# Four places for residual rows, attention-time norms on GpSimd, and a last query block whose exponents are all split in PSUM

## The chip, the cores and the metric

The kernel runs on one core of a Trainium2 chip. The metric is the device time of one execution, in microseconds (us); the median of three runs stands for a kernel. The engines are called as in the profile: PE (TensorE, with its weight loads as PEld), DVE (VectorE), ACT (ScalarE), POOL (GpSimd) and SP (SyncE, which here only issues DMAs).

## The reference

`x` has shape (2, 2048, 512), `cond` (2, 512). A transformer block with conditioned norms is followed by a graph attention over the label mask `adj` of shape (2, 2048, 2048, 11). Cut to what matters here:

```python
# transformer block
h = _ada_ln(x, cond, Wln1, bln1)          # layer norm * (1 + scale) + shift, from cond
q, k, v = heads(h @ Wq + bq), heads(h @ Wk + bk), heads(h @ Wv + bv)   # 16 heads of 32
attn = softmax(einsum('bhqd,bhkd->bhqk', q, k) / sqrt(32))             # 2048 x 2048
x = x + einsum('bhqk,bhkd->bhqd', attn, v).reshape(B, L, D) @ Wo + bo
h = _ada_ln(x, cond, Wln2, bln2)
x = x + gelu(h @ W1 + b1) @ W2 + b2       # 512 -> 2048 -> 512
# graph attention: every row attends to the first 20 rows of its batch, in two directions,
# with a bias and a gate from the 11 labels; then output = x + relu(self_feat + both directions)
```

## The kernel before

**How instructions come into order.** The program is written as straight Python, but every engine call goes through a recorder, the class `Order`. For each call it notes what the call reads and writes. `flush()` then plays a list scheduler over all recorded operations: an operation is taken when its inputs are ready by a table of costs (`cost()`) and latencies between engines, the lowest recorded index first within 100 ns. Operations on DVE and POOL that use the port which the two share are planned one after the other, and POOL is made to wait for the DVE operation ahead of it there. The planned order is then what each engine's queue holds, and the chip runs each queue strictly in that order, whatever the real durations are. All instructions are issued from one line of `flush()`, so every row of the profile says L271, and instructions are told apart by the names of their tiles. In the cost table a `tensor_scalar` on POOL stands at `161 + 0.833 * n` ns, which is 588 ns for a row of 512; on DVE it is 455 ns with two pointers as operands.

**Places.** Tiles are mapped by tag to rings of fixed SBUF places (`places()`). The tag "xr" has two, `vf0` and `vf1`. A third tile of that tag has to wait until the first is read out. The tags "el" and, later, the MLP's raw weights "wr" share places (`el2`, `el3`), as do the MLP's "gl" and the places `h4`, `h5`.

**Attention.** There are 32 heads (two batches of 16). A head has 4 query blocks of 512 and 16 key tiles of 128, taken as 32 units of two key tiles. N is the count of all units. For a unit u:

- `scores`: PE writes two score tiles `st` (128 x 512) into one of three PSUM banks each.
- `exponents`: for the first 14 key tiles of a query block ACT writes the exponent to SBUF (`e`, in places `q0` to `q2`).
- `high_parts`: every 4 units a DMA issued by POOL casts `e` to its f16 high part `eh`.
- `low_parts`, 9 units later (LOW): `el = e - eh`, in f16, one share of the columns on DVE and the rest on POOL (0.52 on DVE, 0.8 in the last head).
- `weigh`, 11 units later (WEIGH): PE multiplies `eh` and `el` with the values `va` into the bank `av`.
- For the last two key tiles of a query block (INBANK = 2) the exponent stays in PSUM: ACT casts the high part, DVE subtracts the low part (tile `ep`), and `weigh_apart` does the products 5 units later (XLAG).

At the end of a query block DVE sums and normalizes `av` into `os`, which SP stores. For the next head the row maxima's bounds are made meanwhile: PE makes `mx`, ACT takes `ab`, DVE takes `sums` and `m`; in `largest_rows` POOL makes `hl`, DVE transposes it to `tr`, and SP sends it to the next head's queries.

**Work beside attention.** Each unit also takes some steps of a `Background` generator, with a pace per head. Heads 0 to 16 project the rest of batch 0 and norm and project batch 1 (`second_batch`: four blocks of 512 rows, each with `first_norm`). Heads 17 to 27 make the MLP's modulation, the output weights, the output projection of batch 0 with the residual (`output`), and the second norm of the MLP's first block (`second_norm`). Heads 28 to 31 do the output of batch 1's first twelve heads. `norm_block` subtracts the mean and multiplies by the reciprocal deviation, four rows-tiles of 128 x 512 a block, in place:

```python
V.tensor_scalar(r, r, mv[:, t, 0:1], rs[:, t:t + 1], ALU.subtract, ALU.mult)
```

Then PE transposes the result (`misc<-ident,x`). In `output`, a row tile `xr` of 128 x 512 is loaded one step ahead, POOL adds the bias, DVE adds the projection, and SP stores it (`x<-xr` in the profile); its place is free when the store has landed:

```python
xr = sb("xr", [P, D], F32, f"xr_{b}_{groups[0]}_{t}")
Q.dma_start(out=xr, in_=x[b, ts(t, P), :] if 0 in groups else x1_dram[i][r, :])
```

**After attention** the MLP takes eight blocks of 512 rows, each with its `second_norm`, with the labels and the folded graph weights made beside it; then the graph attention takes 16 pieces.

Of the kernel before, what the change touches and what calls it, by code (L numbers as in the profile page):

```python
# [11 lines left out]
F32 = mybir.dt.float32  # L12
F32R = mybir.dt.float32r
F16 = mybir.dt.float16
# [3 lines left out]
ALU = mybir.AluOpType  # L18
# [4 lines left out]
P = 128  # L23
# [6 lines left out]
NT = S // P  # L30
# [18 lines left out]

INBANK = 2  # L50
XLAG = 5

PACES = {0: 0.9, 1: 1.25, 17: 0.8, 18: 0.5, 27: 0.6}
NEG = 9000000000000000.0
# [312 lines left out]
def places():  # L367

    w = lambda *ranges: [f"w{i}" for a, b in ranges for i in range(a, b)]
    h = lambda *ranges: [f"h{i}" for a, b in ranges for i in range(a, b)]  # L370
    el = [f"el{i}" for i in range(4)]
    q = [f"q{i}" for i in range(3)]
    plan = {

        "raw": q, "wv": [f"v{i}" for i in range(4)], "wg_a": w((5, 7)),
        "wg_b": ["w1"], "x_a": w((7, 9), (2, 4)), "vs_a": ["w4", "eh2", "w0"],
        "hh0": h((0, 4)), "hl0": h((4, 8)),
        "hh1": ["eh0"], "hl1": ["eh1"], "ones": ["el2"],
        "squares": ["l0"], "g_c": ["l1"], "g_b": ["l2"], "w2": ["vf0", "ab0", "el0", "el1"],
        "bnd": ["h9"], "mag": ["el3"], "part": ["eh2"], "mod_row": ["w9"],  # L380

        "va": w((2, 4), (0, 2)), "va_rest": ["l2", "l3"], "el": el,
        "ab": ["ab0", "ab1"], "sums": ["l0"], "os": ["l4", "l5"],
        "vs": w((4, 5)), "bv": ["vf1"], "bo": w((6, 7)), "qk2": w((15, 17)), "u2": ["h9"],
        "wg": w((5, 7)), "x": w((7, 9)), "uf": ["l1"], "ep": ["ep0", "ep1"],
        "m2": ["m2_0", "m2_1"], "m1": ["m1_0", "m1_1"], "tr": ["tr_0", "tr_1"],
        "m3": ["m3_0", "m3_1"], "mv": ["mv_0", "mv_1"], "rstd": ["rstd_0", "rstd_1"],
        "bn": ["bn_0", "bn_1"],

        "wo": [f"v{i}" for i in range(4)], "xr": ["vf0", "vf1"], "ob": ["h8", "h9"],  # L390
        "oo2": w((15, 17)), "x1_a": w((7, 9)), "ob_b": ["l0"], "oo2_b": ["v2"],

        "w": w((4, 6), (7, 9), (2, 4), (14, 15), (11, 13), (9, 10), (15, 17), (10, 11), (13, 14),
               (0, 2)),
        "w8": ["eh0", "eh1"], "w16": q, "gh": h((0, 4), (8, 9)), "gl": h((4, 8), (9, 10)),
        "x1": ["v0", "v1"], "wr": ["ab0", "ab1"] + el[2:4], "gf": el[0:2],
        "g2": ["eh2"], "b2": w((6, 7)), "res": el[2:4] + ["ab0", "ab1"],

        "wbl": ["l0"], "ai": ["l1", "vf0", "vf1"], "af": ["l2"], "cv": ["l3"], "lab1": ["l4", "l5", "l6", "l7"],
        "cvt": ["v3"], "oo": ["v2"],  # L400
        "fw": ["vf0", "vf1"], "fv": ["ab0", "ab1"], "fs": ["v2"], "fq": ["l0", "l1", "l2", "l3"],
        "ws": w((4, 6)), "wq": h((0, 2)), "ft": h((2, 4)),
        "kbd": ["l4", "l5", "l6", "l7"], "gc": ["l4", "l5", "l6", "l7"], "kv": ["v3"], "kh": ["m1_0", "m1_1"],

        "x2t": ["vf0", "vf1", "ab0", "ab1"], "oos": ["l0", "l1", "l2", "l3"], "sc": ["v0", "v1", "v2"],
        "rwr": ["v3"], "gar": ["h2"], "gmx": ["mv_0", "mv_1"], "gsm": ["tr_0", "tr_1"], "o": el[2:4],
    }
    return plan
# [3 lines left out]
def transformer_then_graph_attention(  # L412
# [267 lines left out]

    HOLD = "hold"

    def norm_block(ps, xt, ln, b, name, hi, lo, stats=None):


        if stats is None:
            for mv, rs in statistics(lambda t: xt[t // 2][:, t % 2, :], 4, name):
                yield
        else:
            mv, rs = stats  # L690
        for t in range(4):
            r = xt[t // 2][:, t % 2, :]
            V.tensor_scalar(r, r, mv[:, t, 0:1], rs[:, t:t + 1], ALU.subtract, ALU.mult)
            if t % 2:
                yield
        for c in range(KC):
            pt = ps()
            for t in range(4):
                T.transpose(pt[:, ts(t, P)], xt[t // 2][:, t % 2, ts(c, P)], ident)
            A.activation(pt, pt, AF.Identity, bias=mods[:, ln, KC + c, b:b + 1],  # L700
                         scale=mods[:, ln, c, b:b + 1])
            split(hi(c), lo(c), pt, A, V)
            yield HOLD if c == 0 else None
# [10 lines left out]
    def first_norm(b, tb, ps, xt, fast, to, stats=None):  # L714
        to[b, tb] = features(b, tb, tb % 2 if fast else 0, "")
        hi, lo = to[b, tb]
        yield from norm_block(ps, xt, 0, b, f"a{b}_{tb}", lambda c: hi[c], lambda c: lo[c],
                              stats)
        for v in range(2 if b == 0 else 0):
            if fast and tb % 2:  # L720
                Q.dma_start(out=h_dram[b][tb][v].rearrange("c p t -> p c t"), in_=whole[v].bitcast(F32))
            else:
                for c in range(KC):
                    Q.dma_start(out=h_dram[b][tb][v, c], in_=to[b, tb][v][c].bitcast(F32))
# [137 lines left out]
    gates = {}  # L862
    pe = {}
    va, m2s, sts, avs, mxs = {}, {}, {}, {}, {}
    es, ehs, els, parts = [], [], {}, {}

    def put(dst, src, low):

# [81 lines left out]

    def split_tiles(u):

        return min(2, max(0, NT - INBANK - u % 8 * 2))

    def exponents(i):
        u = i // 2
        if i % 2 >= split_tiles(u):
            st = sts.pop(i)
            gates[u] = A.activation(st, st, AF.Exp, scale=SCALE)
            t = parts[i] = sb("ep", [P, 2, TB], F16, f"ep_{i}")  # L960
            split(t[:, 0], t[:, 1], st, A, V)
            return
        gates[u] = A.activation(es[u // EQ % 3][:, u % EQ, ts(i % 2, TB)], sts.pop(i), AF.Exp,
                                scale=SCALE)

    def high_parts(i):

        n = sum(split_tiles(i * EQ + k) for k in range(EQ)) * TB
        e, eh = (t[i % 3].rearrange("p u c -> p (u c)") for t in (es, ehs))
        G.dma_start(out=eh[:, 0:n], in_=e[:, 0:n])  # L970

# [18 lines left out]
                     stop=stop and q == 3, skip_group_check=True)  # L990

    def weigh_apart(u):
        for i in range(2 * u + split_tiles(u), 2 * u + 2):
            t = parts.pop(i)
            with order.together("PE"):
                add(avs[0], u // NU, i % NT, t[:, 0], t[:, 1])

    def weigh(u):
        n, qb, kp = u // NU, u % NU // 8, u % 8
        b, h = heads[n]  # L1000
        g, hh = h // 4, h % 4
        nt = split_tiles(u)
        if nt == 0:
            return
        last = kp == 7 or split_tiles(u + 1) == 0
        eh, el = ehs[u // EQ % 3][:, u % EQ], els.pop(u)
        if kp == 0:
            avs[0] = bank("av", [P, 4, VC + 1], F32, f"av_{n}_{qb}")
        av = avs[0]
        with order.together("PE"):  # L1010
            for a in range(nt):
                add(av, n, 2 * kp + a, eh[:, ts(a, TB)], el[:, ts(a, TB)], kp == a == 0,
                    last and a == nt - 1)
        if not last:
            return
        o = sb("os", [P, 4, HD], F32, f"os_{n}_{qb}")
        V.tensor_reduce(o, av[:, :, 1:VC].rearrange("p q (v d) -> p q d v", v=2), AX.X, ALU.add)
        rec = av[:, :, VC]
        V.reciprocal(rec, av[:, :, 0])
        V.tensor_tensor(o, o, rec.unsqueeze(2).to_broadcast([P, 4, HD]), ALU.mult)  # L1020
        Q.dma_start(
            out=o_dram[b][g][ts(qb, TB), ts(hh, HD)].rearrange("(t p) f -> p t f", p=P), in_=o)
# [30 lines left out]
    def attend(n, work=None):  # L1053

        for u in range(n * NU, (n + 1) * NU):
            i, m = u % NU, u + NU
            for a in range(2):
                exponents(2 * u + a)
                if 2 * u + a + 3 < 2 * N:
                    scores(2 * u + a + 3)  # L1060
# [5 lines left out]
                largest(m)  # L1066
            if u % EQ == 0 and u:
                high_parts(u // EQ - 1)
            if u >= LOW:
                low_parts(u - LOW)  # L1070
            if u >= WEIGH:
                weigh(u - WEIGH)
            if u >= XLAG:
                weigh_apart(u - XLAG)
            if m < N and i in (NU // 2 - 1, NU - 1):
                largest_rows(n + 1, i // (NU // 2))
            loads(u)
# [17 lines left out]
    def output(ps, b, groups, bo_b, tail=""):  # L1095
# [3 lines left out]
        def loaded(t):  # L1099
            i, r = b * NTB + t // 4, ts(t % 4, P)  # L1100
            ob = sb("ob" + tail, [P, ng, P], F32, f"ob_{b}_{groups[0]}_{t}")
            for k, g in enumerate(groups):
                Q.dma_start(out=ob[:, k, :], in_=o_dram[b][g][ts(t, P), :])
            xr = sb("xr", [P, D], F32, f"xr_{b}_{groups[0]}_{t}")
            Q.dma_start(out=xr, in_=x[b, ts(t, P), :] if 0 in groups else x1_dram[i][r, :])
            return ob, xr

# [90 lines left out]
    def second_norm(ps, i, xtag):  # L1198
# [6 lines left out]
        def new(to, name):  # L1205
# [1 line left out]
            return to[-1]  # L1207

        yield from norm_block(ps, xt, 1, i // NTB, f"m{i}", lambda c: new(hi, "gh"),
                              lambda c: new(lo, "gl"))  # L1210


    h1 = {}
# [124 lines left out]
    for u in range(N - WEIGH, N):  # L1338
        if u + WEIGH - LOW < N:
            low_parts(u + WEIGH - LOW)  # L1340
        weigh(u)
        if u + WEIGH - XLAG < N:
            weigh_apart(u + WEIGH - XLAG)
    work.rest()


# [483 lines left out]
```

## Time and profile before

| | |
|---|---|
| median of three runs | 3217.29 us (3211.15, 3221.28, 3217.29) |
| the profiled execution | 3220.79 us, of which the profile's span is 3219.0 us |
| mean granted TensorE clock in it | 0.986 |
| PE busy | 3055.7 us, 95% |
| DVE, ACT, POOL busy | 75%, 66%, 43% |
| attention | to about 2126 us |
| MLP and what runs beside it | from there to about 2910 us |
| graph attention | from there to the end |

A row of the timeline is: start, duration, engine, line, operation, output from inputs, the shape, the number of instructions merged into the row, and in brackets how long the engine had been idle before it and what ended that. A row of the form view gives the shortest, median and longest duration in ns. "PEclk" is the share of full speed that the clock gate granted. Busy times of PE are modelled ends of pipelined matmuls.

### The profile page before, as it was taken

What the parts mean: (1) busy time and instruction counts of PE and PEld (TensorE: products, weight loads), DVE (VectorE), ACT (ScalarE), POOL (GpSimd) and SP (SyncE); (2) the same over time, 40 slices, a digit from 0 to 9 for tenths busy, and PEclk for the clock granted to TensorE, in tenths of its full rate; (3) what the DMA queues carried; (4) which work ended last, traced back from release to release, by engine and by line L of the source; (5) the groups of instructions that cost most, each with busy time, mean ns of one, the idle gap of its engine ahead of it and who ended that gap; (6) DMA issues with size and microseconds to landing.
All of it is one profiled execution on the core that took longest, in us unless ns stands there. A gap on an engine that the chain in (4) does not pass through costs nothing.

```text
span 3219.0 us, 75753 instructions
## 1 busy us (share of the span) xinstructions
PE 3055.7 (95%) x28042; PEld 2096.1 (65%) x28042; DVE 2421.9 (75%) x5508; ACT 2132.2 (66%) x4233; POOL 1376.2 (43%) x1440
## 2 busy tenths in 40 slices
PE   7999989999999999999989989989999999999999
PEld 5555555555556555555555555568888887789998
DVE  6688878988889999899989999875576534235665
ACT  5788889999999999999989999842112212112221
POOL 2154545555555666666666656641000000002232
PEclk9999999999999999999999999999999999999999
DMA  8889998797979888899888778874122134132111
GB/s 287 248 210 257 246 227 215 175 227 174 207 169 212 185 173 182 180 205 203 190 187 176 163 150 192 190 222 145 29 66 67 60 105 150 29 98 78 64 58 55
DMA packets 353313, 519.33 MB, mean 161 GB/s; under 512 B 127407, under 2 KB 233431, under 8 KB 336558
## 3 DMA queue, kind: packets, MB, share of 16 engines
q0 software_dynamic: 36864, 234.90, 37.8%
q1 hardware_dynamic: 316078, 279.59, 28.3%
q8 instruction: 220, 3.60, 0.4%
q14 instruction: 151, 1.24, 0.1%
HBM read 187.97 MB, written 91.45 MB: 87 GB/s over the span
## 4 chain that ended last, share of the span: by engine, by line
PE 46%; ACT 4%; DVE 3%; issue 2%; DMA 2%; POOL 1%; SPq 0%; ACTq 0%; POOLq 0%; DVEq 0%
PE ph L271 11%; PE po_s L271 8%; PE gp L271 5%; PE misc L271 5%; PE av L271 4%; PE st L271 4%; PE gs L271 4%; PE mx L271 3%; PE po_x L271 3%; ACT e L271 2%; ACT ab L271 1%; DVE el L271 1%; PE pg L271 1%; DVE sums L271 1%; POOL el L271 1%
## 5 line engine op out<-in xcount | busy, mean ns | idle before, releaser
L271 POOL TENSOR_TENSOR el<-e,eh 128x496 f16<-128x496 f32 (+1 forms) x896 | 991.4, 1120 | 541.2 <-DVE el L271 201.5
L271 ACT ACTIVATE e<-st 128x512 f32<-128x512 f32 x1792 | 1040.7, 643 | 80.8 <-PE st L271 48.3
L271 DVE CUSTOM_DVE_ANT_0 sums<-mx,ab 128x512 bf16<-128x512 f32 x1024 | 700.1, 684 | 146.2 <-ACT ab L271 119.0
L271 PE MATMUL st<-qst,kst 98*128 98x512 f16 x2048 | 698.5, 385 | 50.3 <-DVE ep L271 20.2
L271 DVE TENSOR_TENSOR el<-e,eh 128x528 f16<-128x528 f32 (+1 forms) x896 | 735.2, 845 | 5.8 <-DMA eh<-e 3.0
L271 ACT ACTIVATE ab<-mx 128x512 f32<-128x512 f32 x1024 | 662.3, 647 | 42.3 <-PE mx L271 39.5
L271 PEld LDWEIGHTS <-eh 128*128 128x128 f16 x7168 | 468.3, 97 | 144.8 <-issue 95.1
L271 PE MATMUL av<-va,el 128*128 128x33 f16 x7168 | 510.7, 179 | 25.8 <-DVE el L271 18.2
L271 PE MATMUL av<-va,eh 128*128 128x65 f16 x7168 | 531.9, 192 | 2.5 <-DVE os L271 2.1
L271 PEld LDWEIGHTS <-el 128*128 128x128 f16 x7168 | 438.5, 96 | 129.0 <-DVE el L271 39.8
L271 PE MATMUL mx<-kst,qst 96*128 96x512 f16 x1024 | 388.7, 382 | 27.0 <-DVE m L271 24.3
L271 PE MATMUL mx<-ust,qst 96*128 96x512 f16 x1024 | 391.7, 383 | 21.6 <-ACT ab L271 13.8
L271 ACT ACTIVATE gf<-ph,b_c 128x512 f32<-128x512 f32 x128 | 88.2, 689 | 467.8 <-PE ph L271 411.8
L271 PEld LDWEIGHTS <-qst 96*128 96x128 f16 x2048 | 195.5, 98 | 288.7 <-issue 169.6
L271 PE MATMUL ph<-gh,w 128*128 128x512 f32 x1024 | 344.1, 398 | 3.8 <-ACT w L271 2.8
L271 PEld LDWEIGHTS <-kst 98*128 98x128 f16 x2048 | 168.1, 99 | 220.2 <-issue 173.5
L271 PE MATMUL po_s<-w,g 128*128 128x512 f32 x1152 | 295.6, 397 | 0.0
L271 POOL TENSOR_TENSOR res<-res,b_b 128x512 f32<-128x512 f32 x32 | 42.2, 1337 | 513.7 <-DVE g L271 243.3
L271 PEld LDWEIGHTS po_s<-w,g 128*128 128x128 f32 x1152 | 213.8, 188 | 48.4 <-issue 0.8
L271 DVE CAST g<-gf 128x512 fp32r<-128x512 f32 x128 | 56.0, 438 | 250.1 <-PE po_x L271 240.0
L271 POOL DMA_DIRECT2D eh<-e x256 | 145.9, 570 | 186.5 <-ACT e L271 88.2
L271 PEld LDWEIGHTS ph<-gh,w 128*128 128x128 f32 x1024 | 191.8, 188 | 49.0 <-ACT w L271 3.3
(259 smaller groups left out, 4642.0 us busy)
## 6 DMA issues: line engine op xcount, KB each, us to landing
eh<-e POOLq DMA_DIRECT2D x128, 1024.0 KB, 8.2
eh<-e POOLq DMA_DIRECT2D x128, 768.0 KB, 7.9
wg<-w SPq DMA_DIRECT2D x50, 512.0 KB
x<-in_x SPq DMA_DIRECT2D x24, 512.0 KB
qst<-qk SPq DMA_DIRECT2D x192, 64.0 KB
kst<-qk SPq DMA_DIRECT2D x192, 64.0 KB
x<-xr SPq DMA_DIRECT2D x48, 256.0 KB
v<-vs SPq DMA_DIRECT2D x32, 260.0 KB
```

Source lines behind the costliest of these rows:

```text
L271: ins = call(*args, **kw)
```

## The change

It has three parts.

1. In `output`, the rows of batch 0 use a new tag "xr_a" with four places: `vf0`, `vf1`, `h4`, `h5`. Batch 1 keeps "xr" with `vf0` and `vf1`. Each tag keeps its own turn, but a place that two tags name is one place.
2. `norm_block` takes the engine as an argument. The subtract-and-multiply goes to POOL in `first_norm` of batch 1 (4 blocks, 16 instructions) and in every `second_norm` (8 blocks, 32 instructions). The norms of batch 0, ahead of attention, stay on DVE.
3. In the last query block (the last LAST = 8 units) all 16 key tiles are treated as the last two were: exponent in PSUM, cast on ACT, subtraction on DVE. The results go to two tiles `ep_last` in the places of `e`, since the ring "ep" has only two. The products are made 2 units behind (LASTLAG) into a bank of their own, `x2`. Seven `el` units and two of the casting DMAs drop out; 14 casts on ACT and 14 subtractions on DVE come in. In this block the `low_parts` of earlier units move ahead of the exponents where a new tile begins.

On PE 7 rows fewer are recorded (46434 for 46441, matmuls and others together), DVE has 5415 for 5437, ACT 4240 for 4226, POOL 1449 for 1434, SP 1552 for 1553. Up to the first norm of batch 1, some 466 us into the span, the order on every engine is unchanged.

```diff
--- before.py
+++ after.py
@@ -49,6 +49,8 @@
 
 INBANK = 2
 XLAG = 5
+
+LAST, LASTLAG = 8, 2
 
 PACES = {0: 0.9, 1: 1.25, 17: 0.8, 18: 0.5, 27: 0.6}
 NEG = 9000000000000000.0
@@ -387,7 +389,7 @@
         "m3": ["m3_0", "m3_1"], "mv": ["mv_0", "mv_1"], "rstd": ["rstd_0", "rstd_1"],
         "bn": ["bn_0", "bn_1"],
 
-        "wo": [f"v{i}" for i in range(4)], "xr": ["vf0", "vf1"], "ob": ["h8", "h9"],
+        "wo": [f"v{i}" for i in range(4)], "xr": ["vf0", "vf1"], "xr_a": ["vf0", "vf1"] + h((4, 6)), "ob": ["h8", "h9"],
         "oo2": w((15, 17)), "x1_a": w((7, 9)), "ob_b": ["l0"], "oo2_b": ["v2"],
 
         "w": w((4, 6), (7, 9), (2, 4), (14, 15), (11, 13), (9, 10), (15, 17), (10, 11), (13, 14),
@@ -680,7 +682,7 @@
 
     HOLD = "hold"
 
-    def norm_block(ps, xt, ln, b, name, hi, lo, stats=None):
+    def norm_block(ps, xt, ln, b, name, hi, lo, stats=None, eng=V):
 
 
         if stats is None:
@@ -690,7 +692,7 @@
             mv, rs = stats
         for t in range(4):
             r = xt[t // 2][:, t % 2, :]
-            V.tensor_scalar(r, r, mv[:, t, 0:1], rs[:, t:t + 1], ALU.subtract, ALU.mult)
+            eng.tensor_scalar(r, r, mv[:, t, 0:1], rs[:, t:t + 1], ALU.subtract, ALU.mult)
             if t % 2:
                 yield
         for c in range(KC):
@@ -715,7 +717,7 @@
         to[b, tb] = features(b, tb, tb % 2 if fast else 0, "")
         hi, lo = to[b, tb]
         yield from norm_block(ps, xt, 0, b, f"a{b}_{tb}", lambda c: hi[c], lambda c: lo[c],
-                              stats)
+                              stats, V if b == 0 else G)
         for v in range(2 if b == 0 else 0):
             if fast and tb % 2:
                 Q.dma_start(out=h_dram[b][tb][v].rearrange("c p t -> p c t"), in_=whole[v].bitcast(F32))
@@ -862,7 +864,7 @@
     gates = {}
     pe = {}
     va, m2s, sts, avs, mxs = {}, {}, {}, {}, {}
-    es, ehs, els, parts = [], [], {}, {}
+    es, ehs, els, parts, ends = [], [], {}, {}, []
 
     def put(dst, src, low):
 
@@ -950,6 +952,8 @@
 
     def split_tiles(u):
 
+        if u >= N - LAST:
+            return 0
         return min(2, max(0, NT - INBANK - u % 8 * 2))
 
     def exponents(i):
@@ -957,7 +961,8 @@
         if i % 2 >= split_tiles(u):
             st = sts.pop(i)
             gates[u] = A.activation(st, st, AF.Exp, scale=SCALE)
-            t = parts[i] = sb("ep", [P, 2, TB], F16, f"ep_{i}")
+            t = parts[i] = (sb("ep", [P, 2, TB], F16, f"ep_{i}") if u < N - LAST else
+                            ends[-1][:, u % EQ, i % 2])
             split(t[:, 0], t[:, 1], st, A, V)
             return
         gates[u] = A.activation(es[u // EQ % 3][:, u % EQ, ts(i % 2, TB)], sts.pop(i), AF.Exp,
@@ -966,6 +971,8 @@
     def high_parts(i):
 
         n = sum(split_tiles(i * EQ + k) for k in range(EQ)) * TB
+        if n == 0:
+            return
         e, eh = (t[i % 3].rearrange("p u c -> p (u c)") for t in (es, ehs))
         G.dma_start(out=eh[:, 0:n], in_=e[:, 0:n])
 
@@ -990,10 +997,23 @@
                      stop=stop and q == 3, skip_group_check=True)
 
     def weigh_apart(u):
+        n, qb, alone = u // NU, u % NU // 8, u >= N - LAST
+        if alone and u % 8 == 0:
+            avs[1] = bank("x2", [P, 4, VC + 1], F32, f"av_{n}_{qb}")
         for i in range(2 * u + split_tiles(u), 2 * u + 2):
             t = parts.pop(i)
             with order.together("PE"):
-                add(avs[0], u // NU, i % NT, t[:, 0], t[:, 1])
+                add(avs[alone], n, i % NT, t[:, 0], t[:, 1], alone and i % NT == 0,
+                    alone and i % NT == NT - 1)
+        if alone and u % 8 == 7:
+            weighed(n, qb, avs[1])
+
+    def apart_products(u):
+
+        if 0 <= u - XLAG < N - LAST:
+            weigh_apart(u - XLAG)
+        if N - LAST <= u - LASTLAG < N:
+            weigh_apart(u - LASTLAG)
 
     def weigh(u):
         n, qb, kp = u // NU, u % NU // 8, u % 8
@@ -1011,8 +1031,12 @@
             for a in range(nt):
                 add(av, n, 2 * kp + a, eh[:, ts(a, TB)], el[:, ts(a, TB)], kp == a == 0,
                     last and a == nt - 1)
-        if not last:
-            return
+        if last:
+            weighed(n, qb, av)
+
+    def weighed(n, qb, av):
+        b, h = heads[n]
+        g, hh = h // 4, h % 4
         o = sb("os", [P, 4, HD], F32, f"os_{n}_{qb}")
         V.tensor_reduce(o, av[:, :, 1:VC].rearrange("p q (v d) -> p q d v", v=2), AX.X, ALU.add)
         rec = av[:, :, VC]
@@ -1054,6 +1078,9 @@
 
         for u in range(n * NU, (n + 1) * NU):
             i, m = u % NU, u + NU
+            if u >= N - LAST and u % EQ == 0:
+                low_parts(u - LOW)
+                ends.append(sb(f"q{u // EQ % 3}", [P, EQ, 2, 2, TB], F16, f"ep_last_{u}"))
             for a in range(2):
                 exponents(2 * u + a)
                 if 2 * u + a + 3 < 2 * N:
@@ -1066,12 +1093,11 @@
                 largest(m)
             if u % EQ == 0 and u:
                 high_parts(u // EQ - 1)
-            if u >= LOW:
+            if u >= LOW and not (u >= N - LAST and u % EQ == 0):
                 low_parts(u - LOW)
             if u >= WEIGH:
                 weigh(u - WEIGH)
-            if u >= XLAG:
-                weigh_apart(u - XLAG)
+            apart_products(u)
             if m < N and i in (NU // 2 - 1, NU - 1):
                 largest_rows(n + 1, i // (NU // 2))
             loads(u)
@@ -1101,7 +1127,7 @@
             ob = sb("ob" + tail, [P, ng, P], F32, f"ob_{b}_{groups[0]}_{t}")
             for k, g in enumerate(groups):
                 Q.dma_start(out=ob[:, k, :], in_=o_dram[b][g][ts(t, P), :])
-            xr = sb("xr", [P, D], F32, f"xr_{b}_{groups[0]}_{t}")
+            xr = sb("xr" if b else "xr_a", [P, D], F32, f"xr_{b}_{groups[0]}_{t}")
             Q.dma_start(out=xr, in_=x[b, ts(t, P), :] if 0 in groups else x1_dram[i][r, :])
             return ob, xr
 
@@ -1207,7 +1233,7 @@
             return to[-1]
 
         yield from norm_block(ps, xt, 1, i // NTB, f"m{i}", lambda c: new(hi, "gh"),
-                              lambda c: new(lo, "gl"))
+                              lambda c: new(lo, "gl"), eng=G)
 
 
     h1 = {}
@@ -1339,8 +1365,7 @@
         if u + WEIGH - LOW < N:
             low_parts(u + WEIGH - LOW)
         weigh(u)
-        if u + WEIGH - XLAG < N:
-            weigh_apart(u + WEIGH - XLAG)
+        apart_products(u + WEIGH)
     work.rest()
```

## The prediction

> **What bounds the kernel now.** I read the page first: busy shares, slices, the chain of waits. All instructions are recorded by one helper, so every row says L271 and I go by tile names.
>
> ```profile
> PE 3055.7 (95%) x28042; PEld 2096.1 (65%) x28042; DVE 2421.9 (75%) x5508; ACT 2132.2 (66%) x4233; POOL 1376.2 (43%) x1440
> PE   7999989999999999999989989989999999999999
> PE 46%; ACT 4%; DVE 3%; issue 2%; DMA 2%; POOL 1%; SPq 0%; ACTq 0%; POOLq 0%; DVEq 0%
> ```
>
> TensorE is the bound: nothing but a hole in PE's row can be won. Next the windows, by stage (busy us with counts of PE, weight loads, DVE, ACT, POOL; then granted clock, DMA share, GB/s).
>
> ```profile
> 150.00:1600.00 1450.00, 1365.31 (x15981) 818.35 (x15979) 1284.62 (x2930) 1338.29 (x2728) 854.40 (x909) 0.99 0.89 202
> 1605.00:1625.00 20.00, 13.59 (x116) 7.39 (x113) 12.96 (x31) 11.95 (x26) 9.49 (x11) 0.83 0.65 150
> 1845.00:1860.00 15.00, 7.31 (x65) 4.11 (x65) 14.23 (x21) 9.48 (x18) 6.93 (x8) 0.66 0.40 82
> 2095.00:2150.00 55.00, 43.59 (x479) 32.99 (x476) 38.07 (x62) 25.11 (x48) 28.69 (x34) 0.91 0.76 204
> 2200.00:2900.00 700.00, 700.00 (x3178) 565.59 (x3177) 336.54 (x902) 143.30 (x212) 45.97 (x38) 1.00 0.26 79
> ```
>
> From 2200 on PE has no hole, so the 28 norms of the MLP's later blocks can't matter. In attention DVE, ACT and PE are all near 90%. Three short stretches hold the losses: PE idle 6.4, 7.7 and 11.4 us; and after each hole the granted clock falls, which costs busy time times (1 - clock): 2.3, 2.5 and 3.9 us. A stall's price is so about 1.35 times its idle time (8.7/6.4, 10.2/7.7), and the three places cost 8.7, 10.2 and 15.3 us. The change's three parts aim at just these.
>
> **Part 1, four row places.** The timeline of SyncE's queue (SPq) and of POOL at the first hole; the bracket is the idle time before and what ended it.
>
> ```profile
> 1600.91 0.38 SPq L271 DMA_DIRECT2D x<-xr  x1
> 1609.50 0.34 SPq L271 DMA_DIRECT2D xr<-in_x  x1
> 1615.45 1.26 POOL L271 TENSOR_TENSOR xr<-xr,bo_b 128x512 f32<-128x512 f32 x1 [6.24 <-DMA xr<-in_x]
> 1619.07 0.21 DVE L271 STREAM_TRANSPOSE tr<-hl 128x32 f16<-128x32 f16 x1 [6.10 <-POOL hl L271]
> ```
>
> A row's load waits 8 us on SP for the store out of the same place; POOL waits for the row; hl and two els stand behind POOL, the transpose of hl holds DVE, and DVE's sums hold PE. With four places the loads of batch 0's rows 14 and 15 go ahead in the new instruction order, and hl comes before any of them. But that order now puts the load of batch 1's first row, which keeps the old two places, directly behind that same store, and its bias add on POOL (1.27 us) about five operations after the old blocking point, some 6 us later. SP will wait again, with the ob loads and a store behind it; what is left for POOL is 0 to 3 us of the 6.2. Bounds: the whole 8.7 gone, or 2 us worse if el and the eh cast behind it are needed sooner than hl was. I take -6.
>
> **Part 2, norms on GpSimd.** The second hole:
>
> ```profile
> 1847.60 7.49 DVE L271 TENSOR_SCALAR x<-x,mv_m,rs_m 128x512 f32<-128x512 f32 x4
> 1848.45 5.44 POOL L271 TENSOR_TENSOR el<-e,eh 128x496 f16<-128x496 f32 x5
> 1855.74 0.58 PE L271 MATMUL st<-qst,kst 98*128 98x512 f16 x1 [5.64 <-DVE ep L271]
> ```
>
> One of DVE's four norms takes 6.12 us: it runs only when POOL's row of five els is over. The subtractions (ep) behind it free no score bank, and PE stands. On POOL the norm can't be locked out so: -10.2. The 16 norms of batch 1 took 11.9 us on DVE, up to 1.8 us per block over the 455 ns each that the scheduler assumes; PE waits for x there by some 1.5 us in sum. Removed altogether: 11.7 us.
>
> Added: 20 norms on POOL inside attention (4 blocks of batch 1, MLP block 0), and 28 under a full PE. No row shows this operation on POOL. The nearest are these (min/median/max ns):
>
> ```profile
> L271 POOL TENSOR_SCALAR wo_raw<-wo_raw,vmul x4: 1559/1568/2035, 1323.9 to 1341.5; 128x512 f32<-128x512 f32 x4
> L271 POOL TENSOR_TENSOR xr<-xr,bo_b x32: 1257/1270/1310, 1356.9 to 2126.8; 128x512 f32<-128x512 f32 x32
> L271 DVE TENSOR_SCALAR x<-x,mv_m,rs_m x32: 527/544/6119, 1847.6 to 2734.7; 128x512 f32<-128x512 f32 x32
> ```
>
> The first is the same instruction and shape with one operation in place of two: I take 1.57 us; ends 0.54 (DVE's row) and 2.04 (the slowest of four). The scheduler's own cost table puts 588 ns there, so a block of four ends 4 x 0.98 = 3.9 us later than planned. PE runs in order, and its transposes of x stand in its queue among the scores; before, they follow the norm within 0.1 to 0.4 us. Behind the norms on POOL stand els (needed by PE a median 3.2 us after they end), an eh cast and in two blocks hl, on which DVE's transpose waits with almost no slack. So lateness reaches PE, unless POOL, 59% busy here, starts ahead of its plan. Between all and nothing covered I take half: 2 us x 1.35 x 5 blocks = 13. Part 2: -11.7 + 13 = +1.3 (from -11.7 to +27). DVE is relieved of 20 norms, but DVE els beside POOL work stretch from 0.70 to 1.39 us (at 1604.5); 31 us more POOL in 1900 gives some of it back. I count both at nothing.
>
> One rule speaks to this price from both sides. The Trainium skill, "GPSIMD Engine Reference", section 4.1, sends elementwise work to VectorE, though one-input operations are called roughly line rate, and section 3.1 gives 769 ns for 512 elements at best. By that figure, as an estimate, a block would be 0.7 us late and part 2 would be -7. The row of 1.57 us is what this chip did, and I go by it.
>
> **Part 3, the last query block split in PSUM.** The tail before:
>
> ```profile
> 2113.68 4.91 DVE L271 TENSOR_TENSOR el<-e,eh 128x816 f16<-128x816 f32 x4
> 2119.36 0.21 PE L271 MATMUL av<-va,el 128*128 128x33 f16 x1 [2.56 <-POOL el L271]
> 2122.01 0.62 ACT L271 CAST w<-wr 128x512 fp32r<-128x512 f32 x1 [12.21 <-DMA wr<-in_W]
> 2121.61 2.83 DVE L271 TENSOR_TENSOR el<-e,eh 128x816 f16<-128x816 f32 x3
> 2128.57 0.89 SPq L271 DMA_DIRECT2D wr<-in_W  x2
> 2134.32 0.50 PE L271 MATMUL ph<-gh,w 128*128 128x512 f32 x1 [2.75 <-ACT w L271]
> ```
>
> The last exponent ends at 2108.4; then the DMA cast eh (8 us) and seven els at 1.1 us keep PE at 9.8 of 15 us until 2125, and the weight loads, whose places are els, come only at 2128.57. Removed: 7 DVE els (7.7 us), 7 on POOL (4), two casts. Added: 14 ACT casts (0.49 us pitch, 6.9 us) and 14 DVE subtractions (0.61, 8.5). DVE's work from 2101.1: 7 els of the block before x 1.1, 16 x 0.61, 3.2 of others = 20.7, so the last product is ready at 2122, not 2124.4; ACT, with 39 x 0.49 = 19 us, ends before that. PE's first hole (5.2 us and 4.0 of clock in 2110 to 2130) shrinks by some 2.5 us; the weights' places come free near 2114, so the second hole (4.7 us in 2130 to 2145) goes but for what is left to the first gelu: 4. Sum -6.5. Bounds: -11 (both holes gone); -2 if the score banks, now held until DVE's subtraction, throttle the block.
>
> **Sum.** -6 + 1.3 - 6.5 = -11.2 on the profiled 3220.8 us: 3209.6. That execution lies 3.5 above the median, so 3217.3 - 11.2 = 3206.
>
> **Rivals.** *No change (0.20):* nothing of the 3.9 us is covered: 3.9 x 1.35 x 5 = 26.4; -6 + 14.7 - 6.5 = +2.2, 3219.5. For it: transposes with no slack; against: POOL's idle time. If batch 1's row takes over the whole stall of part 1, the forecast ends here too, at 3212. *Slower (0.22):* the norm with two pointers and two operations takes 2.04 us or more on POOL. Uncovered it stalls PE at the five blocks by 4 x 1.45 = 5.8 us: 39 - 11.7 - 12.5 = +15, 3232. It decides from 1.84 us per norm (5.0 us a block) on. For it: the planner's 588 ns, hl behind the norms; against: only one of four rows is so slow. *Forecast (0.58):* 3206, own range 3195 to 3212.
>
> **Chances.** About 0.3%, 9.7 us, is what a measurement of this kernel can tell from no change. Forecast: 0.50 faster, 0.08 within; no change: 0.04, 0.14, 0.02 slower; slower: 0.03 within, 0.19. Faster 0.54, same 0.25, slower 0.21. The range runs from the forecast with a full gain in parts 1 and 3 (3193) to nearly the slower rival (3231).
>
> **What would show it.** Right: no POOL wait of 6 us for xr near 1610; no DVE instruction above 3 us near 1850; five stretches with x on POOL at 1.5 to 1.6 us and PE gaps of 1 to 3 us at misc<-ident,x; the first gelu 10 to 15 us earlier, counted from the last block's first exponent. Wrong: POOL's x above 1.84 us; gaps of 5 us and clocks below 0.9 near 470, 620, 765, 915 and 1850; a wait of xr for its load again, with hl or els behind it; DVE full and PE no denser in the last 40 us of attention.

## The result, and the profile after

The changed kernel takes 3223.78 us, median of nine runs (3222.24 to 3234.69); the kernel before took 3215.59 us beside it (3210.05 to 3221.28). The ratio is 1.0034, 95% interval 1.0021 to 1.0047: slower by some 11 us by the ratio (8 by the medians), about what the prediction called measurable. The forecast was 3206.

From the page of the changed kernel: busy shares, PE's slices, and the chain of waits.

```profile
PE 3056.4 (95%) x28042; PEld 2097.2 (65%) x28042; DVE 2393.4 (74%) x5467; ACT 2136.0 (66%) x4247; POOL 1469.1 (46%) x1479
PE   7999989999999999999999999989999999999999
PE 18%; DVE 0%; POOL 0%; DMA 0%; issue 0%; SPq 0%; DVEq 0%; POOLq 0%
```

POOL works 93 us more, DVE 28 us less, and the holes that were aimed at look filled in the slices. Against the page of before, DVE has 41 instructions fewer and POOL 39 more (48 norms, 14 subtractions, 7 els on each engine, two casting DMAs), ACT 14 more and PE as many as before; these are the profile's counts, which differ for PE, DVE and POOL from those given with the change. The chain covers under a fifth of the span here, so nothing is read from it. The page doesn't show a loss. The windows do (busy us with counts of PE, weight loads, DVE, ACT, POOL; granted clock, DMA share, GB/s): first three of the changed kernel for the stretches shown of before, then 450 to 960, where batch 1 is normed.

```profile
1605.00:1625.00 20.00, 18.89 (x204) 10.76 (x204) 18.18 (x42) 17.59 (x37) 14.92 (x16) 1.00 0.84 188
1845.00:1860.00 15.00, 9.21 (x99) 4.81 (x98) 9.76 (x23) 11.32 (x21) 11.91 (x10) 0.70 0.53 107
2095.00:2150.00 55.00, 47.48 (x517) 36.17 (x516) 43.60 (x74) 37.22 (x68) 24.18 (x27) 0.97 0.69 200
450.00:960.00 510.00, 473.57 (x5319) 291.02 (x5318) 426.00 (x958) 457.15 (x932) 307.68 (x314) 0.96 0.82 187
```

And the last of them in the kernel before:

```profile
450.00:960.00 510.00, 479.77 (x5459) 295.47 (x5458) 444.75 (x1002) 470.79 (x955) 283.27 (x307) 0.99 0.84 192
```

In 450 to 960 the changed kernel starts 140 matmuls fewer, at a clock of 0.96 instead of 0.99; in the 25 us from 465, 615, 760 and 910, where the four blocks are normed, the clock is 0.80, 0.86, 0.80 and 0.80 (before: 0.96, 1.00, 0.86 and 1.00). Its timeline of POOL and PE at the first norm of batch 1:

```profile
461.78 8.25 POOL L273 TENSOR_SCALAR x<-x,mv_all,rs_all 128x512 f32<-128x512 f32 x4
463.91 0.33 PE L273 MATMUL misc<-ident,x 128*128 128x128 f32 x1 [0.40 <-POOL x L273]
465.97 0.33 PE L273 MATMUL misc<-ident,x 128*128 128x128 f32 x1 [1.51 <-POOL x L273]
468.03 0.33 PE L273 MATMUL misc<-ident,x 128*128 128x128 f32 x1 [1.29 <-POOL x L273]
470.08 0.47 PE L273 MATMUL misc<-ident,x 128*128 128x128 f32 x1 [1.51 <-POOL x L273]
```

Four norms take 8.25 us, where the planner has 2.35, and PE waits for each. The form view of the changed kernel gives the price (min/median/max ns):

```profile
L273 POOL TENSOR_SCALAR x<-x,mv_m,rs_m x32: 2057/2076/2644, 1852.3 to 2740.4; 128x512 f32<-128x512 f32 x32
L273 POOL TENSOR_SCALAR x<-x,mv_all,rs_all x16: 2062/2065/2914, 461.8 to 921.6; 128x512 f32<-128x512 f32 x16
```

To see where time is lost and won, I took from both traces the start of the same matmul, the n-th `st` in attention and then the n-th gelu, and subtracted (changed minus before, us):

| matmul or gelu | before at | after minus before | lies behind |
|---|---|---|---|
| st 256 | 401.4 | -3.6 | same order of instructions; chance |
| st 832 | 1004.3 | +10.0 | the four norm blocks of batch 1: +13.6 |
| st 1472 | 1576.2 | +9.1 | |
| st 1536 | 1641.6 | +2.7 | the hole near 1610, gone: -6.4 |
| st 1728 | 1816.6 | +1.5 | |
| st 1792 | 1884.6 | +3.8 | MLP block 0's norm: +2.3 |
| st 2031 | 2096.1 | +1.9 | |
| gelu 0 | 2140.0 | -12.7 | |
| gelu 16 | 2244.2 | -2.8 | the last block, net: -4.7 |
| gelu 96 | 2728.1 | +1.4 | one stall in the MLP: +4.2 |

The table compares one execution of each kernel. The eight other traces with batch 1's norms on VectorE lie between -4.1 and +0.7 us of this execution of before from st 256 to 832, so +13.6 stands clear of chance, but not to the microsecond. The -6.4 at st 1536 belongs to that execution, as the last runs below show.

The loss in the MLP is a place that the prediction had declared free. One of the seven blocks normed there puts its norms on POOL ahead of `fs<-fw,fs`, the low part of a folded weight, and the next load of `fw` comes too late (timeline, changed kernel):

```profile
2611.47 8.41 POOL L273 TENSOR_SCALAR x<-x,mv_m,rs_m 128x512 f32<-128x512 f32 x4
2621.10 1.30 POOL L273 TENSOR_TENSOR fs<-fw,fs 128x512 fp32r<-128x512 f32 x1
2626.34 1.06 PE L273 MATMUL misc<-kvx,fw 128*128 128x40 f32 x8 [2.46 <-DMA fw<-in_WselfT]
```

### The profile page after: what moved, and what is told of

It reads as the page before. It is cut to its first block, busy times and chain, and to the rows that moved or that the text cites. A ratio compares the mean times of both kernels' runs of the same rounds, so it can differ in the third digit from the quotient of the medians.

```text
span 3220.4 us, 75768 instructions
## 1 busy us (share of the span) xinstructions
PE 3056.4 (95%) x28042; PEld 2097.2 (65%) x28042; DVE 2393.4 (74%) x5467; ACT 2136.0 (66%) x4247; POOL 1469.1 (46%) x1479
## 5 line engine op out<-in xcount | busy, mean ns | idle before, releaser
L273 DVE TENSOR_TENSOR el<-e,eh 128x528 f16<-128x528 f32 (+1 forms) x889 | 727.6, 843 | 1.7 <-PE av L273 1.4
L273 PE MATMUL ph<-gl,w 128*128 128x512 f32 x512 | 203.0, 396 | 0.0
```

What stands on the lines that cost most here:

```text
L273: ins = call(*args, **kw)
```

## The experiments

Theory P says that the norm on GpSimd costs 2.07 us where the plan has 0.59, and PE stands behind it; the rest of the change is a gain. Theory R says that any re-planned order has waits of its own. "Parts" are those of the change. Ratios are against the kernel before, run beside each.

**All norms back on VectorE: parts 1 and 3 (norms_dve).**

```diff
-                              stats, V if b == 0 else G)
+                              stats)
-                              lambda c: new(lo, "gl"), eng=G)
+                              lambda c: new(lo, "gl"))
```

> The changed kernel with all norms back on VectorE: parts 1 and 3 alone. Theory P (price): the norm on GpSimd takes 2.07 us where the planner has 0.59, and PE stands behind it; by the progress of PE through the two traces (start of the same score matmul in both) that costs 13.6 us at the four blocks of batch 1, 2.3 net at MLP block 0 and 4.2 in the MLP, 20 in all, while the rows gain 6.4 and the last block 4.7. It expects 3215.6 - 11 = 3204.5, ratio 0.9965, the 6.1 us norm near 1850 back, and no hole near 2624. Rival R (re-planning): any re-planned order has its own new waits, and the last block's split costs more than it gives; it expects 3218 or more.

Measured: 3204.65 us, ratio 0.9969 (0.9957 to 0.9981). That is P's number to 0.2 us, in part by luck, for the uncertainty is 4 us; the norm of 6.1 us is back (525/540/6120 ns in the form view), and near 2611 no hole is left. Part 2 costs the difference of the two ratios, 0.0065, some 21 us, uncertain by 6; parts 1 and 3 gain 10.

**Part 2 alone (only_norms).** The kernel before with the engine given to `norm_block`.

```diff
-    def norm_block(ps, xt, ln, b, name, hi, lo, stats=None):
+    def norm_block(ps, xt, ln, b, name, hi, lo, stats=None, eng=V):
-            V.tensor_scalar(r, r, mv[:, t, 0:1], rs[:, t:t + 1], ALU.subtract, ALU.mult)
+            eng.tensor_scalar(r, r, mv[:, t, 0:1], rs[:, t:t + 1], ALU.subtract, ALU.mult)
-                              stats)
+                              stats, V if b == 0 else G)
-                              lambda c: new(lo, "gl"))
+                              lambda c: new(lo, "gl"), eng=G)
```

> The kernel before with part 2 alone. Theory P expects 3215.6 + 20 = 3236 (ratio 1.006), PE waiting for x in five blocks of attention. Rival R expects no more than the whole change showed, 3224 or less.

Measured: 3243.2 us, ratio 1.0083 (1.0066 to 1.0101). R as it was put, with the last block at fault, is out: the loss goes with the norms. The time is 7 us worse than P's number. In its trace batch 1 costs 13.1 us of PE's progress between the table's marks, MLP block 0 2.1, the stretch from the last scores to gelu 16 6.1, and `fw` 3.7; the third wasn't in P's sum, and the run has a hole of 6.4 us in it, at a transpose of `ob` near 2176, whose cause is not shown.

**The planner is told the price (priced).**

```diff
-        return (36 + 0.83 * n, 0.0) if not ins else (161 + 0.833 * n, 0.0) \
+        return (36 + 0.83 * n, 0.0) if not ins else (161 + (0.833, 2.75, 3.72)[pointers] * n, 0.0) \
```

> The changed kernel, with the planner's cost of a POOL tensor_scalar set by operands to 1.57 us (one pointer) and 2.07 us (two pointers). Only the order moves. Theory P, as a plan that believes the wrong duration: the scheduler puts other work ahead of the transposes, half of the 20 us comes back: about 3214. Theory P, as plain load (the work is too long for its place whatever the order): 3222 to 3225. Rival R: no direction, within 5 of 3224.

Measured: 3214.02 us, ratio 0.9997 (0.9987 to 1.0008). The same instructions on the same engines, in another order, are as fast as the kernel before: some 12 us less than the changed kernel. The norms are no faster (a block takes 8.62 us here), but the transposes are queued later, and the timeline of the first block shows PE without a wait for x:

```profile
465.85 8.62 POOL L273 TENSOR_SCALAR x<-x,mv_all,rs_all 128x512 f32<-128x512 f32 x4
468.28 0.27 PE L273 MATMUL misc<-ident,x 128*128 128x128 f32 x1
470.73 0.27 PE L273 MATMUL misc<-ident,x 128*128 128x128 f32 x1
472.46 0.33 PE L273 MATMUL misc<-ident,x 128*128 128x128 f32 x1
```

PE's waits for the norms follow the plan and the price. These are the rows of the waits view for 450 to 960 (us in total, times, longest), in this order: the changed kernel, the run with one operation that comes next, this run, and the kernel before:

```profile
PE misc L273 <- POOL x L273: 14.2, 12, 1.7
PE misc L273 <- POOL x L273: 8.1, 10, 1.2
PE misc L273 <- POOL x L273: 1.6, 2, 1.0
PE misc L271 <- DVE x L271: 1.0, 2, 0.7
```

The other 9 of the 21 us stay. Against the trace of the changed kernel, PE's progress in this one is 10.0 us better in batch 1, 6.4 at MLP block 0 and 2.2 in the MLP from gelu 16 to 96. It is 5.3 us worse from st 1216 to 1472, 4.7 from st 1792 to 2031 and 3.9 from there to gelu 16: the new order loses time of its own there, as theory R says of any. So even with its price in the plan GpSimd was no better place for these norms than VectorE; how much of the 9 us is load on POOL and how much the new order is not shown.

**One operation instead of two (one_op).**

```diff
-            eng.tensor_scalar(r, r, mv[:, t, 0:1], rs[:, t:t + 1], ALU.subtract, ALU.mult)
+            eng.tensor_scalar(r, r, mv[:, t, 0:1], None if eng is G else rs[:, t:t + 1], ALU.subtract,
+                              *([] if eng is G else [ALU.mult]))
```

> The changed kernel whose GpSimd norms only subtract the mean and leave out the multiplication by the reciprocal deviation: one operation and one pointer in place of two; nothing else moves. Theory P expects the norm at 1.57 us, as in the one-pointer row of the weights, and the loss to shrink with the overrun, (1.57 - 0.59) / (2.07 - 0.59) = 0.66 of 20 us: 3217. If the price follows the two inputs and not the operations, the norm stays at 2.07 us. Rival R expects 3224.

Measured: 3216.68 us, ratio 1.0001 (0.9991 to 1.0012). The form view gives the norm without its multiplication:

```profile
L273 POOL TENSOR_SCALAR x<-x,mv_all x16: 1552/1560/2021, 467.7 to 921.8; 128x512 f32<-128x512 f32 x16
```

1.56 us, the price of the weights' row in the kernel before, which also has one operation and one pointer. The second operation with its pointer costs 0.5 us more. The time falls with the price, by some 10 us against the changed kernel by the ratios (0.0033, uncertain by 5), where P expected 7. The clean comparison is batch 1, where the order is that of the changed kernel: 6.8 us lost instead of 13.6. From about 1850 on the order is another after all, since this norm of MLP block 0 no longer waits for the reciprocal deviation, and PE has a hole of 5.6 us near 2080 that the changed kernel doesn't have.

**Part 1 alone (rows_only).** The kernel before with the tag "xr_a" (`vf0`, `vf1`, `h4`, `h5`).

```diff
-            xr = sb("xr", [P, D], F32, f"xr_{b}_{groups[0]}_{t}")
+            xr = sb("xr" if b else "xr_a", [P, D], F32, f"xr_{b}_{groups[0]}_{t}")
```

> The kernel before with part 1 alone. By the progress of PE through the trace of parts 1 and 3 (from +1.5 us at score matmul 1472 to -5.0 at 1536) the rows are worth 6.5 us: 3214.3 - 6.5 = 3208, ratio 0.998, and no hole near 1614. If the store awaited by batch 1's first row takes over the stall, 3214.

Measured: 3212.7 us, ratio 0.9986 (0.9974 to 0.9999): a gain of 4.5 us with an interval from 0.3 to 8.4, and by the medians 1.4, so between the two expectations.

**Part 3 alone (last_only).** The kernel of parts 1 and 3 with two places for both batches.

```diff
-            xr = sb("xr" if b else "xr_a", [P, D], F32, f"xr_{b}_{groups[0]}_{t}")
+            xr = sb("xr", [P, D], F32, f"xr_{b}_{groups[0]}_{t}")
```

> The kernel before with part 3 alone. By the progress of PE in the run of parts 1 and 3 (from -8.1 us at score matmul 2031 to -15.2 at the MLP's gelu 16) the last block is worth 7.1 us; in the changed kernel it was 4.7. Expected: 3214.3 - 7 = 3207, ratio 0.998. With the rows the two should sum to the 9.7 us (3204.6) of both together, or up to 13.5. If the split only trades the wait for the score banks against the wait for the weights, 3214.

Measured: 3206.49 us, ratio 0.9977 (0.9967 to 0.9986), 7.4 us, as expected. But this kernel has two row places, and its trace has no hole near 1610 (nor has that of part 2 alone). What I had read as a fixed stall was perhaps an event. The kernel before was therefore traced twice more.

**The kernel before again (before_a, before_b).**

> The kernel before, unchanged, once more, for its trace. In the first trace the store x<-xr at 1600.9 took 8 us to land and cost 7 to 8 us of PE. Theory S (the hole is built into two places): it is here again near 1610. Theory E (an event of one execution: the two other runs with two places, part 2 alone and part 3 alone, got the next row's load out 2 us after the same store, with the same order on SP): no hole over 2 us between 1600 and 1630. The hole of 5.6 us near 1850 is there in both.

> The same as the run ahead of it, a further execution: theory S has the hole near 1610, theory E has none; the one near 1850 is there.

Measured: one run each, 3211.3 and 3213.54 us. Neither has a hole there; SyncE's queue in the first of them, with the same store and the load behind it:

```profile
1595.61 0.38 SPq L272 DMA_DIRECT2D x<-xr  x1
1598.05 0.34 SPq L272 DMA_DIRECT2D xr<-in_x  x1
```

The load leaves 2.1 us after the store's issue ended, not 8.2. So of five traces with two places one has the hole: theory E holds. From st 1472 to 1536, where the run of part 1 alone gains 6.5 us on the first trace, these two gain 6.9 with two places: the traces show no gain by the four places here, and what its 4.5 us come from is not shown. PE's hole of 5.64 us behind VectorE's norm of MLP block 0, by contrast, is in all three traces of before, and at 4.96 to 5.74 us in every other one that norms this block on VectorE.

**Only batch 1's norms on GpSimd (b1_pool), only those of MLP blocks 1 to 7 (mlp_pool)**, both with parts 1 and 3.

```diff
-                              stats)                              # b1_pool
+                              stats, V if b == 0 else G)
-                              lambda c: new(lo, "gl"))            # mlp_pool
+                              lambda c: new(lo, "gl"), eng=G if i else V)
```

> Parts 1 and 3, with only the 16 norms of batch 1 on GpSimd, at the planner's wrong price; the MLP's norms stay on VectorE. Theory P has the largest term of the loss here: 13.6 us by PE's progress in the changed kernel's trace (from -3.6 us at score matmul 256 to +10.0 at 832); 3204.7 + 13.6 = 3218, ratio 1.001, norms of 2.07 us. If the loss belongs to the MLP's norms, 3205 to 3208.

Measured: 3218.92 us, ratio 1.0006 (0.9997 to 1.0016), theory P's number; in its trace PE again loses 13.6 us from st 256 to 832.

> Parts 1 and 3, with only the norms of MLP blocks 1 to 7 on GpSimd (28 of the 48), planner's price as in the change. The prediction counted these at nothing. By the changed kernel's trace one of the seven blocks puts 8.4 us of norms ahead of fs<-fw,fs in POOL's queue, PE waits 2.5 us for fw near 2624 and loses 4.2 with the clock: 3204.6 + 4.2 = 3209, ratio 0.998. If they are covered, 3204.6.

Measured: 3208.62 us, ratio 0.9985 (0.9975 to 0.9995); PE's hole at `misc<-kvx,fw` is there, 2.12 us, and from gelu 16 to 96 PE loses 5.3 us, where parts 1 and 3 lose 0.0. Against parts 1 and 3 (0.9969) these are 0.0037 and 0.0016, so 12 and 5 us of the 21; each is uncertain by some 5. What is left for MLP block 0 is 4, a difference within its uncertainty.

**Only MLP block 0 on GpSimd, with its price in the plan (m0_priced).** Parts 1 and 3, and the cost line of the run "priced".

```diff
-                              lambda c: new(lo, "gl"))
+                              lambda c: new(lo, "gl"), eng=V if i else G)
```

> Parts 1 and 3, with only MLP block 0's norm on GpSimd (the one place where VectorE was locked out, 6.1 us) and its price in the planner set to 2.07 us; batch 1 and MLP blocks 1 to 7 stay on VectorE. Theory P: in the run with the right price PE gained 4.2 us at this place (from -1.4 at score matmul 1728 to -5.6 at 1792), where with the wrong price it lost 2.3; so 3204.6 - 4.2 = 3200, ratio 0.9957. If load and not the plan decides, 3205 to 3207.

Measured: 3209.51 us, ratio 0.9980 (0.9969 to 0.9990): not better than parts 1 and 3, and not clearly worse. At the place itself the trace does what was expected: PE has no hole of 5 us, and gains 3.9 us there (from -12.3 at st 1728 to -16.2 at st 1792). But by st 2031 it stands at -13.1: in the re-planned order behind it PE stands 2.1 us near 2066, and the clock falls to 0.67 in 2070 to 2080. And from st 2031 to gelu 16 it gains 1.3 us, where parts 1 and 3 gain 7.2. The gain was won and given back by the order behind it.

**VectorE's norm of block 0 in another form (m0_stt).** Parts 1 and 3.

```diff
-            eng.tensor_scalar(r, r, mv[:, t, 0:1], rs[:, t:t + 1], ALU.subtract, ALU.mult)
+            if name == "m0":
+                V.scalar_tensor_tensor(r, r, mv[:, t, 0:1], rs[:, t:t + 1].to_broadcast([P, D]),
+                                       ALU.subtract, ALU.mult)
+            else:
+                eng.tensor_scalar(r, r, mv[:, t, 0:1], rs[:, t:t + 1], ALU.subtract, ALU.mult)
```

> Parts 1 and 3, all norms on VectorE, but the four of MLP block 0 as scalar_tensor_tensor with the reciprocal deviation as a broadcast second input, in place of tensor_scalar. If the 6.1 us are a lock that this form of tensor_scalar meets while POOL works (theory L), the new form runs at 0.7 to 1.4 us beside POOL's els, the 5.6 us hole of PE near 1844 goes, and the time falls by 4 to 7 us: 3198 to 3201. If any VectorE operation on SBUF is held there, the hole stays and the time is 3204.7.

Measured: 3199.69 us, ratio 0.9949 (0.9937 to 0.9960), the best of all. The number is as theory L had it, and the theory is wrong: the new form is held beside POOL's els just the same. Its form view:

```profile
L273 DVE SCALAR_TENSOR_TENSOR x<-x,mv_m,rs_m x4: 741/744/6179, 1835.5 to 1843.0; 128x512 f32<-128x512 f32 x4
```

And its timeline of DVE and POOL. The second of the four norms starts at 1836.19, just ahead of POOL's row of five els, and ends at 1842.37, 0.56 us after that row:

```profile
1835.53 8.17 DVE L273 SCALAR_TENSOR_TENSOR x<-x,mv_m,rs_m 128x512 f32<-128x512 f32 x4
1836.38 5.43 POOL L273 TENSOR_TENSOR el<-e,eh 128x496 f16<-128x496 f32 x5
```

PE's hole is still 4.96 us, and PE's progress over that place doesn't gain (-12.1 to -11.3). Why this kernel is 0.002 better than parts 1 and 3 is not shown. The intervals touch, and traces of the kernel before itself lie up to 10 us apart. The two profiled executions differ by 5.1 us in span, and by 6.9 already at st 256, where the order of instructions is the same.

## Why the prediction was wrong

**What bounds it: right in kind, wrong in one inference.** PE is the bound and the holes are what counts. "From 2200 on PE has no hole, so the 28 norms of the MLP's later blocks can't matter" failed: a window without holes shows that what is queued now is covered, not that 8.4 us more on POOL would be. Behind the norms stood `fs<-fw,fs` and, behind that, the load of `fw`: 5 us, counted at nothing.

**Part 1: the term was an event.** The -6 was sized on an 8 us wait that one trace in five shows. The profiled 3220.8 us lay toward the slow end of its kernel's runs for this reason, among others. That batch 1's first row would now stand behind the same store was right: in the changed kernel SyncE waits 3.2 us there, and POOL doesn't, since its bias add comes later in the queue. Measured: -4.5, interval -8.4 to -0.3.

**Part 2: the term that turned the sign.** Forecast +1.3, measured +21. Three of its steps failed.

The first is the price: 1.57 us from a row with one operation. The row's slowest case, 2.04, stood as the upper end; 2.07 is what every norm takes, so a block is late by 4 x 1.48 = 5.9 us, not 3.9. The cover, taken as half, was about right: half of 5.9 with the factor 1.35 is 4.0 a block, and batch 1 lost 13.6 us in four blocks, 3.4 each. The price alone would not have turned the sign of the whole: put into the prediction's own sum it gives 5 x 4.0 - 11.7 = +8.3 for part 2, and some 3213 in all.

The second is the credit of 10.2 us at MLP block 0. With 4.0 us of lateness it should have left -6.2 there; PE's progress shows +2.3, 8.5 us off. The third is the 28 norms counted at nothing, +4.2 there. The three together make the +21 (8.3 + 8.5 + 4.2). In the run whose plan knew the price this place gained 4.2 us, so the credit was lost in good part by the same wrong 0.59 us. The norm that was locked out at block 0 is gone; the timelines of POOL, PE and DVE there, changed kernel:

```profile
1852.30 4.13 POOL L273 TENSOR_SCALAR x<-x,mv_m,rs_m 128x512 f32<-128x512 f32 x2
1857.64 4.12 POOL L273 TENSOR_SCALAR x<-x,mv_m,rs_m 128x512 f32<-128x512 f32 x2
1859.76 0.48 PE L273 MATMUL misc<-ident,x 128*128 128x128 f32 x1 [2.50 <-POOL x L273]
1863.04 0.21 DVE L273 STREAM_TRANSPOSE tr<-hl 128x32 f16<-128x32 f16 x1 [6.37 <-POOL hl L273]
```

PE waits for x, and DVE waits 6.4 us for hl, which stands behind the norms on POOL: a queue order that the prediction had named for two blocks of batch 1 and not looked for here. In 1845 to 1860 PE gained 1.9 us of 15 and the clock stayed at 0.70.

The Trainium skill's figure, 769 ns at best for 512 elements (GPSIMD Engine Reference, section 3.1), is 2.7 times below the 2.07 us that this instruction takes here, and the prediction was right to leave it out of the sum. Its estimate of -7 by that figure lets nothing be covered; with half covered, as in the sum, it would be -9.3.

**Part 3: right.** -6.5 forecast, -7.4 measured alone (-10.6 to -4.5). The last subtraction of the changed kernel ends near 2124.8 (2122 was forecast), DVE nearly full up to it; the first gelu starts 12.7 us earlier, 14.6 counted from st 2031, just ahead of the last block (10 to 15 was forecast), and most of that is given back by gelu 16. The waiting for score banks that was the lower bound is there and small (timeline, PE):

```profile
2108.50 0.38 PE L273 MATMUL st<-qst,kst 98*128 98x512 f16 x1 [1.46 <-DVE ep_last L273]
```

**The rivals.** The slower rival had the mechanism and the price, and decided from 1.84 us. Its 3232 was too high: it let nothing be covered, +27 at the five blocks where 16 were measured, and like the forecast it had the MLP's other norms at nothing. What happened lies between it and no change. The range's lower end, 3193, does not follow from the prediction's own bounds: 3217.3 - 8.7 + 1.3 - 11 is 3199.

## What to carry to other kernels

Before a step moves to another engine under a written-out order, look up what the planner believes it costs there: here, with 0.59 us in the plan for a 2.07 us instruction, the move cost 21 us, and correcting that one number gave 12 back with no work moved. A new order has waits of its own, so a gain at one place is counted only with what lies behind it. A price is taken from a row with the same number of operations and operands, or its upper end is used for the forecast. A hole in one profile is a term of the sum only when a second execution has it: here the hole tied to the landing of one store was in one trace of three, the one tied to a norm and a row of els in all three.

## What the runs showed of the hardware

A two-operation `tensor_scalar` with two pointers on GpSimd takes 2.07 us for 128 x 512 f32, with one of each 1.56; a `tensor_tensor` of the same shape takes 1.27 (the rows' bias add in the kernel before), so two inputs are cheaper there than two operations with pointers. A VectorE norm that started just ahead of GpSimd's row of five els (5.4 us) lasted until 0.3 to 0.6 us after that row: 6.12 us as `tensor_scalar` and 6.18 us as `scalar_tensor_tensor`, where the medians are 0.54 and 0.74. In three executions of the same program the load behind one store of 256 KB left 8.2, 2.1 and 2.1 us after the store's issue had ended.
